# Second layer's output norms: the residual on GpSimd, sums R behind it, and another order in the last pair of tiles

## The chip, the cores and the metric

The kernel runs on one core of a Trainium2 chip. The core has five engines with a queue of instructions each: TensorE (PE in the profile, with its weight loads as PEld), VectorE (DVE), ScalarE (ACT), GpSimd (POOL) and SyncE (SP), which here only issues transfers. An engine works its queue strictly in order; an instruction waits until the semaphores it names have been raised by other engines or by transfers, and whatever stands behind it on the same engine waits too.

The metric is the device time of one execution in microseconds (us). Three runs of the kernel before took 855.74, 856.96 and 857.38 us, so the median is 856.96 us. The profiled execution took 857.13 us by the same clock, and its span from the first to the last instruction is 855.2 us.

## The reference

The input x has 4 x 512 rows of 512 numbers, that is 2048 rows, all float32. Two layers follow each other, and each adds the layer norm of its result to its own input:

```python
x = x + _layernorm(_L0_attn_ref(_layernorm(x, axis=-1), w_gate, w_up, w_down), axis=-1)
x = x + _layernorm(_L0_ffn_ref(_layernorm(x, axis=-1), W_gate, W_up, W_down), axis=-1)
```

The first layer computes `silu(x Wg^T)`, sets to zero the half of the 1376 entries of each row that are smallest in magnitude, multiplies by `x Wu^T` and by `Wd^T`. The second layer is `(silu(x Wg^T) * (x Wu^T)) Wd^T` with no selection. A layer norm takes away the row's mean and divides by the square root of its variance plus 1e-5. What the change touches is the last step of the second layer only: the layer norm of its result y, and the sum with the residual.

## The kernel before

**Tiles.** 2048 rows are 16 tiles of 128 rows. Layer 1 works on units of two tiles, layer 2 on blocks of four tiles (blocks 0 to 3), so block b has the tiles 4b to 4b+3. Products are formed with fewer matmuls than the plain way, by schemes in which sums of operands are multiplied and sums of products taken; the sums are VectorE, ScalarE and GpSimd work.

**A block of layer 2.** `Block.group` computes 128 hidden columns of gate and up for each of two halves, for each of five groups (a = 0 to 4). A group has 26 products (the table `PRODUCTS`), each of two matmuls (line 814), on six PSUM banks that are used again and again: a bank accumulates, and its running value is read after each product, by ScalarE where an output is begun (line 828) and by VectorE where it is added to (line 824). A product may not be issued into a bank before the readers of the bank's last value are done. So VectorE's place in its queue decides when TensorE may go on. Then ScalarE takes the silu (line 835) and GpSimd multiplies (line 837) and forms sums for the down projection (`down_sums`, lines 185 to 188). The last 96 hidden columns are done by `rest_sevens`; its right operands are four sums R of the block's input, made on GpSimd by `rest_right` (lines 193 to 196, about 1.27 us each), issued in the source behind group 1 of the block. R lives in the four buffers with the tag "y", which the output tiles also use.

**The down projection.** `Block.finish` calls `downs`, which takes pairs of output tiles through seven products p1 to p7, one 640 KB piece of the weights each (tag "wd", three buffers), and a short `rest` matmul pair. In blocks 0 to 2 the order is p1, p5, p6 per pair, then p7, p2, p4, p3 for both pairs together. p4 completes the two tiles yb, p3 the two tiles ya. In block 3 (`final`), p4 and p2 come per pair at the end, with p3 ahead of them for both.

**The output norm.** `out_norm` loads the residual xr (256 KB, tag "xr", two buffers), takes mean and variance (`moments`: lines 170, 172, 174 on VectorE, then `rs`, the power -1/2, on GpSimd, line 176), subtracts the mean (line 466), multiplies by `rs` and adds xr in one VectorE instruction (line 467), and issues the store of the tile (line 469). Only in the very last tile is the left half of y read straight from PSUM (`pa`, line 461).

**Who sets the order.** The source order is not the order of the queues. The block is built with `schedule_with_timeline_sim=True`: a scheduler orders each engine's instructions by its own model of time, and `tc.issue_after(i)` holds work back behind an instruction i. In the built program of before, the norms of tiles 0 and 1 of a block are interleaved on VectorE with the first additions of the next block's group 0, and on GpSimd R0 and R1 stand before the two `rs` of these norms and R2 and R3 behind them.

In the trace, tile and line names are those of the program: `yb` is an output tile of layer 2, `pab`, `pxb`, `pyb` are the six banks of a group, `padb`, `pxdb`, `pydb` the banks of the down projection.

Of the kernel before, what the change touches and what calls it, by code (L numbers as in the profile page):

```python
# [13 lines left out]
ALU = mybir.AluOpType  # L14
# [79 lines left out]
def sandwich_kernel(  # L94
# [18 lines left out]
    nc = tc.nc  # L113
# [47 lines left out]
    def bank(tag, nm):  # L161
        return psum.tile([P, 512], F32, tag=tag, name=nm)
# [165 lines left out]
    def down_right(work, key, k, w_d, nm):  # L328

        t = work.tile([P, HC, H2], F32, tag="wd", name=f"wd{nm}_{k}", bufs=3)  # L330
        raw = dict(p1=(0, 0), p2=(1, 0), p3=(1, 1))
        if k in raw:
            r, c = raw[k]
            src = w_d[r * HF : (r + 1) * HF, c * H2 : (c + 1) * H2]
            src = src.rearrange("(k p) h -> p k h", p=P)
        else:
            src = presums[key][dict(p5=1, p6=2, p7=3, p4=4)[k] - 1]
            src = src.rearrange("p (k h) -> p k h", h=H2)
        nc.sync.dma_start(t, src)
        return t  # L340

    def downs(work, pairs, key, w_d, wr, res, dst, nm, final=False):

        st = []

        ws = {}

        def begin():
            tiles, left, last = pairs[len(st)]
            pa, px, py = [bank(k, f"{k}d{nm}_{tiles[0]}")[:, :H2] for k in ("pa", "px", "py")]
            ya, yb = [
                work.tile([P, H], F32, tag="y", name=f"y{nm}_{t}", bufs=4) for t in tiles
            ]
            st.append((tiles, left, last, pa, px, py, ya, yb))

        def product(k, which, i=None, part=slice(None)):

            if k not in ws:
                ws[k] = down_right(work, key, k, w_d, f"{nm}_{pairs[0][0][0]}")
            first = i is not None
            for p in [st[i]] if first else st[part]:
                for c in range(HC):
                    nc.tensor.matmul(  # L368
                        p[which], p[1](k, c), ws[k][:, c, :],
                        start=first and c == 0, stop=c == HC - 1, skip_group_check=not first,  # L370
                    )

        def rest(ps, p, i, cols, first=False):
            nc.tensor.matmul(
                ps, p[2](i), wr[:, cols], start=first, stop=True, skip_group_check=not first
            )

        lo, hi = slice(H2), slice(H2, H)
        PA, PX, PY = 3, 4, 5
        pz = []  # L380

        def p1(i):
            begin()
            product("p1", PA, i)

        def p6(i):
            product("p6", PX, i)
            tiles, left, last, pa, px, py, ya, yb = st[i]
            nc.scalar.copy(yb[:, lo], pa)
            nc.vector.tensor_add(ya[:, hi], yb[:, lo], px)  # L390

        def p7():
            product("p7", PX)
            for p in st:
                tiles, left, last, pa, px, py, ya, yb = p
                nc.vector.tensor_add(yb[:, hi], yb[:, lo], px)  # L396
                pz.append(bank("pt", f"pz{nm}_{p[0][0]}")[:, :H2])
                rest(pz[-1], p, 1, hi, True)

        def c22():  # L400
            for p, z in zip(st, pz):
                tiles, left, last, pa, px, py, ya, yb = p
                nc.vector.tensor_add(yb[:, hi], yb[:, hi], py)
                nc.vector.tensor_add(yb[:, hi], yb[:, hi], z)

        def p2(part=slice(None)):
            product("p2", PA, None, part)
            for p in st[part]:
                tiles, left, last, pa, px, py, ya, yb = p
                rest(pa, p, 0, lo)  # L410
                if not final:
                    nc.scalar.copy(ya[:, lo], pa)
            if not final:
                c22()
            else:
                for p in st[part]:
                    tiles, left, last, pa, px, py, ya, yb = p
                    if p is st[-1]:
                        out_norm(work, tiles[0], ya, res, dst, nm, pa)
                    else:  # L420
                        nc.scalar.copy(ya[:, lo], pa)
                        out_norm(work, tiles[0], ya, res, dst, nm)

        def p4(part=slice(None)):
            product("p4", PX, None, part)
            for p in st[part]:
                tiles, left, last, pa, px, py, ya, yb = p
                rest(px, p, 1, lo)
                nc.vector.tensor_add(yb[:, lo], yb[:, lo], px)
                out_norm(work, tiles[1], yb, res, dst, nm)  # L430

        def p3(part=slice(None)):
            product("p3", PY, None, part)
            for p in st[part]:
                tiles, left, last, pa, px, py, ya, yb = p
                rest(py, p, 0, hi)
                nc.vector.tensor_add(ya[:, hi], ya[:, hi], py)
                if not final:
                    out_norm(work, tiles[0], ya, res, dst, nm)

        heads = [
            f
            for i in range(len(pairs))
            for f in (lambda i=i: p1(i), lambda i=i: product("p5", PY, i), lambda i=i: p6(i))
        ]
        if not final:
            return heads + [p7, p2, p4, p3]

        ends = [lambda f=f, i=i: f(slice(i, i + 1)) for i in range(len(pairs)) for f in (p4, p2)]
        return heads + [p7, c22, p3] + ends  # L450

    def out_norm(work, t, y, res, dst, nm, pa=None):


        xr = work.tile([P, H], F32, tag="xr", name=f"xr{nm}_{t}")
        nc.sync.dma_start(xr, res[ts(t, P), :])
        if pa is not None:
            parts = [pa, y[:, H2:]]
            mv, rs = moments(parts, f"o{nm}_{t}", "f")
            for i in range(2):  # L460
                nc.vector.tensor_scalar(
                    y[:, ts(i, H2)], parts[i], mv[:, 0:1], None, ALU.subtract
                )
        else:
            mv, rs = moments([y], f"o{nm}_{t}", "o")
            nc.vector.tensor_scalar(y, y, mv[:, 0:1], None, ALU.subtract)
        nc.vector.scalar_tensor_tensor(y, y, rs, xr, ALU.mult, ALU.add)
        queue = nc.sync if pa is None else nc.scalar
        queue.dma_start(dst[ts(t, P), :], y)

# [457 lines left out]
    def layers(nm, general):  # L928
        with ExitStack() as sctx:
            wpool = sctx.enter_context(tc.tile_pool(name="w" + nm, bufs=1))  # L930
            big = sctx.enter_context(tc.tile_pool(name="big" + nm, bufs=10))
            work = sctx.enter_context(tc.tile_pool(name="work" + nm, bufs=2))
# [28 lines left out]
            for q in range(2):  # L961
# [3 lines left out]
                t = [y[:, :, ts(q, Q)] for y in (t1, t2, t4)]  # L965
# [72 lines left out]
            for tag, n in (("wg", 43), ("wu", 43), ("wus0", 10), ("wus1", 10)):  # L1038
                n = min(n, NG * NP - len(w_of))
                t = wpool.tile([P, n, P], F32, tag=tag, name=f"{tag}2{nm}")  # L1040
                i = 0
# [7 lines left out]
            t = wpool.tile([P, 7, 2, n], F32, tag="wus2", name=f"w_rest{nm}")  # L1049
# [18 lines left out]
            for b, block in enumerate(blocks):  # L1068
                last = b + 1 == len(blocks)
                for a in range(HC):  # L1070
                    block.group(a, w_of[a * NP : (a + 1) * NP])
                    block.down_sums(a)
                    if b == 2 and a == 0 and not general:
                        nbad, loads = count_bad()
                    if b and a == 1:
                        block.rest_right()
                if b:
                    block.rest_sevens(rest_left)
                elif general:
                    block.rest(w_rest)  # L1080
                if b == 0:
                    blocks_w = [w[:, 2 * c : 2 * c + 2, :] for w in w_rest for c in range(2)]
                    with tc.issue_after(block.mark):
                        rest_left = stationary_sums(nc.vector, *blocks_w, *w_rests)
                if not last:
                    with tc.issue_after(block.mark):
                        for k in range(TB):
                            blocks[b + 1].norm(k)
                    blocks[b + 1].sums()
                with ExitStack() as order:  # L1090
                    if last and not general:
                        for i in loads:
                            order.enter_context(tc.issue_after(i))
                    block.finish([0, 1], wr, last)
# [43 lines left out]
```

## Time and profile before

| what | value |
|---|---|
| median of three runs | 856.96 us (855.74 to 857.38) |
| profiled execution, its own time | 857.13 us |
| its span | 855.2 us |
| PE busy | 839.8 us, 98% of the span |
| DVE busy | 599.5 us, 70% |
| ACT busy | 347.2 us, 41% |
| POOL busy | 167.2 us, 20% |
| output norms of layer 2, the fused VectorE multiply-add (line 467) | 16 of 0.750 us |
| the subtraction before it (line 466) | 15 of 0.477 us at the median, one of 1.425 us |
| GpSimd operation on 128 x 512 float32 (lines 193 to 196) | 12 of about 1.27 us |

A busy share is an average over stages with different limits. TensorE's busy time counts overlapping and modelled ends, so 98% does not say that it never waits: where two matmul pairs that usually start 0.43 us apart start 1 us apart, TensorE has waited. The trace's timeline gives start and duration of each instruction, and in brackets the idle time before it and what ended it.

### The profile page before, as it was taken

What the parts mean: (1) busy time and instruction counts of PE and PEld (TensorE: products, weight loads), DVE (VectorE), ACT (ScalarE), POOL (GpSimd) and SP (SyncE); (2) the same over time, 40 slices, a digit from 0 to 9 for tenths busy, and PEclk for the clock granted to TensorE, in tenths of its full rate; (3) what the DMA queues carried; (4) which work ended last, traced back from release to release, by engine and by line L of the source; (5) the groups of instructions that cost most, each with busy time, mean ns of one, the idle gap of its engine ahead of it and who ended that gap; (6) DMA issues with size and microseconds to landing.
All of it is one profiled execution on the core that took longest, in us unless ns stands there. A gap on an engine that the chain in (4) does not pass through costs nothing.

```text
span 855.2 us, 10736 instructions
## 1 busy us (share of the span) xinstructions
PE 839.8 (98%) x3550; PEld 640.8 (75%) x3550; DVE 599.5 (70%) x1679; ACT 347.2 (41%) x719; POOL 167.2 (20%) x230
## 2 busy tenths in 40 slices
PE   9999999999999999999999999999999999999996
PEld 5556566767667676677867888888888888888885
DVE  4988679796977768597867665766656665576524
ACT  3367574748466575746122331133211332033200
POOL 1000000100000100000000453154503553055401
PEclk9999999999999999999999999999999999999999
DMA  9996013727324233196466003510055001530032
GB/s 332 385 365 218 1 55 124 253 74 256 132 92 133 89 129 137 62 329 236 167 206 209 1 2 94 201 68 1 2 174 189 2 1 31 167 129 1 1 104 98
DMA packets 65393, 112.20 MB, mean 131 GB/s; under 512 B 4720, under 2 KB 44784, under 8 KB 64432
## 3 DMA queue, kind: packets, MB, share of 16 engines
q1 hardware_dynamic: 65184, 111.16, 38.2%
q8 instruction: 30, 0.49, 0.2%
q14 instruction: 35, 0.29, 0.1%
q10 hardware_dynamic: 144, 0.26, 0.1%
HBM read 90.96 MB, written 20.45 MB: 130 GB/s over the span
## 4 chain that ended last, share of the span: by engine, by line
PE 89%; DMA 3%; DVE 3%; SPq 2%; ACT 1%; issue 1%; POOL 1%; POOLq 0%; DVEq 0%; ACTq 0%
PE pg L541 15%; PE pxb L814 9%; PE pab L814 8%; PE pyb L814 8%; PE pxu L210 6%; PE pxd L368 6%; PE pxdb L368 5%; PE pyd L368 4%; PE pyu L210 4%; PE pad L368 4%; PE pau L210 4%; PE padb L368 4%; PE pydb L368 4%; PE ph L715 2%; PE pxrb L210 1%; SPq L253 1%
## 5 line engine op out<-in xcount | busy, mean ns | idle before, releaser
L593 ACT ACTIVATE ja<-v,cur 128x1376 bf16<-128x1376 f32 x96 | 138.4, 1441 | 42.7 <-DVE cur L618 32.5
L541 PE MATMUL pg<-wg,xT 128*128 128x456 f32 (+1 forms) x384 | 155.3, 549 | 0.3 <-DVE p L563 0.3
L541 PEld LDWEIGHTS pg<-wg,xT 128*128 128x128 f32 x384 | 71.9, 190 | 61.4 <-issue 56.4
L837 POOL TENSOR_TENSOR hTb<-sg,hTb 128x512 f32<-128x512 f32 x40 | 50.9, 1272 | 103.7 <-DVE hTb L824 91.7
L545 ACT ACTIVATE p<-pg 128x456 f32<-128x456 f32 (+1 forms) x48 | 26.1, 548 | 66.0 <-PE pg L541 56.6
L176 POOL TENSOR_TENSOR rs_o<-ve_o,nhalf 128x1 f32<-128x1 f32 x16 | 10.7, 682 | 188.4 <-DVE ve_o L174 188.4
L210 PE MATMUL pau<-wu,xT 128*128 128x344 f32 x128 | 43.1, 452 | 0.0
L835 ACT ACTIVATE sg<-sg 128x512 f32<-128x512 f32 x40 | 23.0, 622 | 48.5 <-DVE sg L824 48.5
L176 POOL TENSOR_TENSOR rs_i<-ve_i,nhalf 128x1 f32<-128x1 f32 x16 | 11.3, 711 | 153.8 <-DVE ve_i L174 93.2
L824 DVE TENSOR_TENSOR sg<-sg,pxb 128x256 f32<-128x256 f32 x80 | 33.6, 420 | 10.4 <-PE pxb L814 8.6
L824 DVE TENSOR_TENSOR hTb<-hTb,pab 128x256 f32<-128x256 f32 x60 | 25.1, 418 | 22.2 <-ACT sg L828 11.0
L368 PE MATMUL pad<-wd_p,hT 128*128 128x256 f32 x160 | 38.9, 380 | 0.2 <-DMA wd_p<-in_L_attn_w_down_dram 0.2
L368 PE MATMUL padb<-wdb_p,hTb 128*128 128x256 f32 x160 | 38.1, 380 | 0.6 <-DMA wdb_p<-in_L_ffn_W_down_dram 0.6
L828 ACT ACTIVATE hTb<-pab 128x256 f32<-128x256 f32 x40 | 15.3, 383 | 55.8 <-PE pab L814 50.5
L368 PE MATMUL pydb<-wdb_p,D 128*128 128x256 f32 x160 | 37.6, 379 | 0.0
L368 PE MATMUL pxd<-wd_p,hT 128*128 128x256 f32 x160 | 37.1, 380 | 0.5 <-DVE y L396 0.5
L368 PE MATMUL pxdb<-wdb_p,hTb 128*128 128x256 f32 x160 | 36.2, 379 | 0.1
L368 PEld LDWEIGHTS pxd<-wd_p,hT 128*128 128x128 f32 x160 | 30.3, 190 | 6.6 <-DVE y L396 0.9
L368 PEld LDWEIGHTS pad<-wd_p,hT 128*128 128x128 f32 x160 | 29.7, 190 | 6.9 <-issue 1.2
L720 ACT COPY hT<-ph 128x512 f32<-128x512 f32 (+1 forms) x45 | 22.6, 509 | 29.3 <-PE ph L715 23.8
L368 PEld LDWEIGHTS padb<-wdb_p,hTb 128*128 128x128 f32 x160 | 30.3, 190 | 5.2 <-DMA wdb_p<-in_L_ffn_W_down_dram 1.0
L210 PEld LDWEIGHTS pau<-wu,xT 128*128 128x128 f32 x128 | 23.8, 190 | 13.6 <-issue 4.3
(299 smaller groups left out, 1920.1 us busy)
## 6 DMA issues: line engine op xcount, KB each, us to landing
wd_p<-sum_a SPq DMA_DIRECT2D x28, 640.0 KB, 4.1
wd_p<-in_L_attn_w_down_dram SPq DMA_DIRECT2D x21, 640.0 KB, 3.9
wdb_p<-sum_f SPq DMA_DIRECT2D x16, 640.0 KB, 4.1
wdb_p<-in_L_ffn_W_down_dram SPq DMA_DIRECT2D x12, 640.0 KB, 4.1
w_ops<-area SPq DMA_DIRECT2D x4, 1664.0 KB, 6.2
xn<-in_x_dram SPq DMA_DIRECT2D x16, 256.0 KB, 4.3
xr<-in_x_dram SPq DMA_DIRECT2D x16, 256.0 KB, 4.1
x<-y SPq DMA_DIRECT2D x16, 256.0 KB, 3.3
```

Source lines behind the costliest of these rows:

```text
L176: nc.gpsimd.tensor_tensor(rs, ve, nhalf, ALU.pow)
L210: nc.tensor.matmul(ps, self.left[k][:, c, :], self.right[k][:, c, :], start=first and c == 0, stop=c == 1, skip_group_check=not first,)
L368: nc.tensor.matmul(p[which], p[1](k, c), ws[k][:, c, :], start=first and c == 0, stop=c == HC - 1, skip_group_check=not first,)
L541: nc.tensor.matmul(pg, self.xT[:, i, c, :], wg[:, c, c0:c1], start=(c == 0), stop=(c == NH - 1),)
L545: nc.scalar.activation(p[:, c0:c1], pg, AF.Silu)
L593: nc.scalar.activation(junk, v, AF.Sign, bias=cur[:, 0, i : i + 1], accum_out=cur[:, 1, i : i + 1],)
L715: nc.tensor.transpose(pt[: isz[i], c, :], h[:, i * P : i * P + isz[i]], ident)
L720: copy(hT[:, g0 : g0 + nf, :], pt[:, :nf, :])
L814: self.product = nc.tensor.matmul(banks[k], w[wv], self.left[xv], start=first, stop=True, skip_group_check=not first,).ins
L824: self.mark = add(c, c, banks[k]).ins
L835: nc.scalar.activation(sg[:, part], sg[:, part], AF.Silu)
L837: nc.gpsimd.tensor_mul(h[:, part], sg[:, part], h[:, part])
```

## The change

It has three parts.

1. In blocks 0 to 2, the norms of the two tiles that p3 completes (six tiles in all: 0, 1, 4, 5, 8, 9) are done differently (`spare`). One VectorE instruction subtracts the mean and multiplies by `rs`, in place of the subtraction alone, and the residual xr is added by GpSimd in place of VectorE's fused multiply-add. VectorE issues one instruction less for each tile, GpSimd one more. The store then waits for GpSimd. The norms of the other ten tiles stay as they were.
2. `rest_right` is held back behind the last instruction of the last output norm (`normed[-1]`). In the built program, GpSimd's order at the three boundaries is now: both `rs`, both residual sums, R0, R1, R2, R3, where it was R0, R1, both `rs`, R2, R3.
3. In block 3, p3 is no longer done for both pairs ahead of p4 and p2, but per pair: p4, p3, p2 of the first pair, then p4, p3, p2 of the second. The weights of p4 are now loaded before those of p3. In the built program TensorE does p4 of pair 0 with its rest, p3 of pair 0 with its rest, eight matmuls of p4 of pair 1, p2 of pair 0 with its rest, the end of p4 of pair 1, p3 of pair 1, p2 of pair 1. The number of matmuls is the same.

On VectorE, the part of a boundary's queue that changes is, for tiles 0 and 1 (and so for 8 and 9; at tiles 4 and 5 the addition from `pab` stands behind the norms' variances):

```
before: add pab, ve0, sub0, ve1, sub1, add pxb, add pab3, fused0, add pyb, fused1, add pxb4
after:  add pab, ve0, ve1, add pxb, add pab3, submul0, submul1, add pyb, add pxb4
```

```diff
@@ downs, p3
                 if not final:
-                    out_norm(work, tiles[0], ya, res, dst, nm)
+                    out_norm(work, tiles[0], ya, res, dst, nm, spare=key == "f")
@@ downs, order of the last block
-        ends = [lambda f=f, i=i: f(slice(i, i + 1)) for i in range(len(pairs)) for f in (p4, p2)]
-        return heads + [p7, c22, p3] + ends
-
-    def out_norm(work, t, y, res, dst, nm, pa=None):
+        ends = [
+            lambda f=f, i=i: f(slice(i, i + 1)) for i in range(len(pairs)) for f in (p4, p3, p2)
+        ]
+        return heads + [p7, c22] + ends
+
+    normed = []
+
+    def out_norm(work, t, y, res, dst, nm, pa=None, spare=False):
@@ out_norm
             mv, rs = moments([y], f"o{nm}_{t}", "o")
-            nc.vector.tensor_scalar(y, y, mv[:, 0:1], None, ALU.subtract)
-        nc.vector.scalar_tensor_tensor(y, y, rs, xr, ALU.mult, ALU.add)
+            if spare:
+                nc.vector.tensor_scalar(y, y, mv[:, 0:1], rs, ALU.subtract, ALU.mult)
+                nc.gpsimd.tensor_add(y, y, xr)
+            else:
+                nc.vector.tensor_scalar(y, y, mv[:, 0:1], None, ALU.subtract)
+        if not spare:
+            nc.vector.scalar_tensor_tensor(y, y, rs, xr, ALU.mult, ALU.add)
+        normed.append(nc.cur_bb.bb.instructions[-1])
@@ layer 2, groups of a block
                     if b and a == 1:
-                        block.rest_right()
+                        with tc.issue_after(normed[-1]):
+                            block.rest_right()
```

## The prediction

> **What bounds the kernel now.** I read the engine totals, then what TensorE waited for, and the timeline where it waited. The first lines are the page's engine totals and the trace's list of waits of PE.
>
> ```profile
> PE 839.8 (98%) x3550; PEld 640.8 (75%) x3550; DVE 599.5 (70%) x1679; ACT 347.2 (41%) x719; POOL 167.2 (20%) x230
> ...
> PE pxb L814 <- DVE hTb L824: 2.0, 3, 1.0
> PE pab L814 <- DVE hTb L824: 0.3, 1, 0.3
> ```
>
> TensorE sets the pace nearly everywhere, so an engine beside it is worth something only where TensorE waits for it. The waits listed are few, and they lie at the three boundaries between blocks, where group 0 of the next block shares VectorE with the norms. The list understates them, because the modelled end of the pair before hides part of a wait; the cadence does not. A group is 26 pairs, and between waits two pairs start 0.43 us apart: from 563.59 to 574.81 the chain shows the same pair of groups 0 and 1 of block 1, 11.22 us apart. Here is the third boundary on the timeline.
>
> ```profile
> 750.27 0.60 PE L814 MATMUL pab<-T,area 128*128 128x256 f32 x2
> ...
> 753.00 1.26 POOL L194 TENSOR_TENSOR R<-xTb,R 128x512 f32<-128x512 f32 x1 [0.65 <-DMA out_dram<-yb]
> ...
> 753.12 1.43 DVE L466 TENSOR_SCALAR yb<-yb,mv_ob 128x512 f32<-128x512 f32 x1
> ...
> 754.23 1.25 POOL L176 TENSOR_TENSOR rs_ob<-ve_ob,nhalf 128x1 f32<-128x1 f32 x2
> 754.47 0.41 DVE L824 TENSOR_TENSOR hTb<-hTb,pxb 128x256 f32<-128x256 f32 x1
> ...
> 754.93 0.70 PE L814 MATMUL pxb<-T,area 128*128 128x256 f32 x2 [1.05 <-DVE hTb L824]
> ...
> 762.81 0.59 PE L814 MATMUL pab<-T,wg 128*128 128x256 f32 x2
> ```
>
> Group 0 takes 762.81 - 750.27 = 12.54 us here, 1.32 more than 11.22. The other boundaries: 552.30 to 564.72 is 12.42 (1.20 more), 651.09 to 663.89 is 12.80 (1.58 more). In the second, a small matmul of the flags (pbad) delays two pairs by 0.21 and 0.11 us, which the change leaves, so 1.26. VectorE costs TensorE 1.20 + 1.26 + 1.32 = 3.78 us.
>
> The chain at the first boundary: the two powers on GpSimd stand behind R1, which waits for a store; VectorE stands at its first multiply-add; the addition that frees the bank pxb is behind it.
>
> ```profile
> 556.73 1.06 POOL L176 TENSOR_TENSOR rs_ob<-ve_ob,nhalf 128x1 f32<-128x1 f32 x2
> ...
> 557.31 0.75 DVE L467 SCALAR_TENSOR_TENSOR yb<-yb,rs_ob,xrb 128x512 f32<-128x512 f32 x1 [1.00 <-POOL rs_ob L176]
> ...
> 557.98 0.41 DVE L824 TENSOR_TENSOR sg<-sg,pyb 128x256 f32<-128x256 f32 x1
> ...
> 559.44 0.70 PE L814 MATMUL pxb<-T,area 128*128 128x256 f32 x2 [0.55 <-DVE hTb L824]
> ```
>
> The end of the kernel, where nothing overlaps:
>
> ```profile
> 846.25 1.00 SPq L456 DMA_DIRECT2D xrb<-x  x1
> ...
> 847.64 0.43 DVE L170 BATCH_NORM_STATS2 st_ob<-padb 128x6 f32<-128x256 f32 x1
> 848.10 0.75 DVE L467 SCALAR_TENSOR_TENSOR yb<-yb,rs_ob,xrb 128x512 f32<-128x512 f32 x1
> 848.76 0.20 DVE L172 BATCH_NORM_AGGREGATE mv_ob<-st_ob 128x2 f32<-128x12 f32 x1
> ...
> 849.90 0.75 DVE L467 SCALAR_TENSOR_TENSOR yb<-yb,rs_ob,xrb 128x512 f32<-128x512 f32 x1
> ```
>
> The last matmuls are done at 847.6; tile 15's multiply-add lies between the last tile's statistics and their aggregation.
>
> **The boundaries, part by part.** Per tile VectorE loses a subtraction (0.477 us) and a multiply-add (0.750) and gets one instruction with two row scalars. The input norms of layer 2 have that form (line 181): 0.546 at the median. So 0.68 us less for each of six tiles, 4.1 in all, but what counts is when the freed additions run. At the first boundary, with durations of before: the first variance ends at 554.79 as now; GpSimd, R gone, starts the power 0.08 later (as 549.21 to 549.29) and needs 0.53 for one (1.06 for two), so the powers end at 555.40 and 555.93. VectorE goes straight on: addition from pxb at 554.76, from pab3 at 555.10 (its product starts at 554.47 and is readable 0.63 later), the new instruction at 555.44 and 555.97, the addition from pyb near 556.4 instead of 557.98. Before, 1.46 us lay between that addition and the pair that waited for it (557.98 to 559.44), so this pair could go at 557.9; by cadence it is due at 552.30 + 14 x 0.432 = 558.35. The other wait, for the addition from pxb (before at 555.55, now 554.76, read by 555.18), is due at 555.76. Both go. The third boundary has the same times 197.97 us later. At the second the three additions from the banks move 0.66 us up, to 653.34 (654.00 before, which let a pair due at 654.00 go at 654.47; now read by 653.76), and the powers, ended near 654.4, are ready before VectorE comes at 654.53. I take the whole 3.78 us. Its ends are 3.78 and 2.0 (three lost races, first rival); I stay near the upper, because VectorE then has nothing left that is late.
>
> What the moved work meets. The two residual sums are GpSimd additions on 128 x 512, the kind and size of R0 to R3: 1.27 us each, from about 556.1 to 558.7. R0 and R1 follow, to 561.3. R2 and R3 wait for the stores of tiles 0 and 1: now issued about 557.5 and 558.8, landed 2.4 later, so R3 ends near 563.9, as before (562.57 + 1.27). Behind them wait the group's multiplication (564.19 before, could now start 1.2 earlier but does not) and the sums for the down projection; their readers are the down products some 40 us on, and R's are the matmuls from 611.1. Cover gone would cost what GpSimd lags, but it is idle most of each group. SP issues the two stores after GpSimd rather than VectorE, about when it did (558.12, 559.11); behind them stand the next residual loads and weights that nobody awaits for tens of us. ScalarE's next read of pyb stands behind VectorE's addition and moves up with it. These cost nothing.
>
> Against the move stands the Trainium skill, "GPSIMD Engine Reference", section "Engine selection": elementwise work belongs on VectorE, GpSimd being about twice as slow with two inputs. The rows agree on the speed (1.27 against 0.75), and by that rule each tile would cost 0.52 more, 3.1 us in all; nobody on TensorE's path waits for these tiles, so I give it nothing.
>
> **The last pair.** TensorE's matmuls are the same number in another order. p4 gets the earlier load (issued 824.73, about 4 us, needed at 831.88), p3 the later one (826.89, needed after 12 matmuls, 834.5), p2 the third (831.64, lands near 835.8, needed at 838.8): no wait. Tile 15's sum is complete after 12 + 12 + 8 + 12 + 4 matmuls at 0.216 us, 842.45, so its norm is done by about 846.6, and the last tile's aggregation follows its statistics at 848.1 instead of 848.76: up to 0.67 us. But the last residual load has two buffers, so it waits for tile 12's multiply-add, which comes near 845.0 (845.05 before); issued at 846.2, landing 3.3 later as this load did, it is there at 849.5, against a multiply-add that could start at 849.23. Landings of these two loads were 2.6 and 3.3 us. The ends are 0 (all else hidden) and 0.67; I take 0.4, by the same load's own row.
>
> **Sum.** 3.78 + 0.4 = 4.18 us off the profiled 857.13 gives 852.95. That execution is 0.17 above the median of the runs, so the median would be 852.8.
>
> **The rivals.**
>
> *GpSimd gets in first.* At 753.12 the subtraction took 1.43 us instead of 0.48, because R1 had begun 0.12 earlier; it ended 0.29 after R1. At 555.41 it was the other way: R1 took 1.36 and the subtraction, 0.25 ahead, its 0.48. The second new instruction has the form of that subtraction, and the first residual sum becomes ready just as it does: VectorE waits for the second power (555.93 + 0.04), GpSimd for the first new instruction (555.99 + 0.08). The margin is 0.10 us, 0.18 at the second boundary. If GpSimd wins, VectorE stands until 556.07 + 1.27 + 0.29 = 557.63, the addition from pyb starts at 557.55, the pair goes near 558.95 instead of 558.35: 0.6 us. At the first and third boundary together 1.2: 854.0; at all three 1.8: 854.6. The Trainium skill, "SBUF — State Buffer", section "Who interferes with whom", gives the rule: VectorE in a two-port mode and GpSimd share a port pair under an exclusive lock, and whichever issues first blocks the other for the whole instruction. The two rows agree with it.
>
> *The norms are not what TensorE waits for.* If another step of group 0 (ScalarE's reads, which stand in the same chain) held these pairs, 3.78 us would stay and the time be 856.5, within 0.2%. Against it: ScalarE's late read at 558.42 waited for VectorE.
>
> *Slower: the sums block the bank additions.* Six GpSimd operations now run without gaps where four ran with them. If each also stopped VectorE's additions from PSUM, each boundary would stand 2 x 1.27 us longer while losing nothing: 3 x 2.54 = 7.6, 860.4. It decides as soon as these additions take longer than 0.42 us. Against it: over all 360 of them the longest is 0.423, and those beside R2 at 560.35 are no longer.
>
> **How the numbers follow.** My case 45%; a lost race at one or two boundaries 33% (up to 854.0), at all three 7% (854.6); unchanged 7%; slower 4% for the blocked additions and 4% for what I do not see. The range: the top is three lost races and nothing at the end (857.0 - 2.0 = 855.0); the bottom the full 4.45 us and the 0.5 us by which runs lie below their median: 852.0. It leaves out about 15%. 0.2% (1.7 us) is about what a measurement of this kernel can tell from no change; the first three cases are faster by more: 0.85 and a little of the fourth.
>
> **What would show it.** Group 0 of blocks 1 to 3 at 11.2, 11.6 and 11.2 us; powers right behind the variances; the new instruction at 0.55, or one of each two near 1.8 where the race is lost; additions from PSUM still 0.42; the last aggregation near 848.1 - 3.8. It is wrong if TensorE in group 0 waits for VectorE as long as before, or if a later group or down product begins to wait for GpSimd.

## The result, and the profile after

The changed kernel took 854.38 us in the median of 12 runs (853.83 to 855.74), the kernel before 856.90 us in 12 runs beside it. The ratio is 0.9972, with a 95% interval of 0.9964 to 0.9980: faster, by 2.5 us. The forecast was 852.8 with a range of 852.0 to 855.0. The profiled execution took 854.17 us, its span is 852.4 us.

First the engine totals on the page of the kernel after, then its list of what PE waited for (us in total, times, longest).

```profile
PE 839.4 (98%) x3550; PEld 641.6 (75%) x3550; DVE 597.6 (70%) x1673; ACT 347.5 (41%) x719; POOL 174.1 (20%) x236
```

```profile
PE pxb L824 <- DVE hTb L834: 0.9, 2, 0.5
```

VectorE has six instructions less and GpSimd six more, as the change says. The waits of PE for VectorE in group 0 went from four to two. Which two were left is in the timeline of the kernel after: the first boundary, the second, the third, and the end.

```profile
554.55 1.21 POOL L176 TENSOR_TENSOR rs_ob<-ve_ob,nhalf 128x1 f32<-128x1 f32 x2 [4.34 <-DVE ve_ob L174]
...
555.18 2.22 DVE L471 TENSOR_SCALAR yb<-yb,mv_ob,rs_ob 128x512 f32<-128x512 f32 x2
...
555.86 1.27 POOL L472 TENSOR_TENSOR yb<-yb,xrb 128x512 f32<-128x512 f32 x1
...
557.33 0.41 DVE L834 TENSOR_TENSOR sg<-sg,pyb 128x256 f32<-128x256 f32 x1
...
558.66 0.70 PE L824 MATMUL pxb<-T,area 128*128 128x256 f32 x2 [0.47 <-DVE hTb L834]
...
653.84 1.00 DVE L471 TENSOR_SCALAR yb<-yb,mv_ob,rs_ob 128x512 f32<-128x512 f32 x2
...
654.51 2.69 POOL L472 TENSOR_TENSOR yb<-yb,xrb 128x512 f32<-128x512 f32 x2 [0.91 <-ACT sg L838]
...
748.24 0.60 PE L824 MATMUL pab<-T,area 128*128 128x256 f32 x2
...
751.44 2.22 DVE L471 TENSOR_SCALAR yb<-yb,mv_ob,rs_ob 128x512 f32<-128x512 f32 x2
...
752.11 1.27 POOL L472 TENSOR_TENSOR yb<-yb,xrb 128x512 f32<-128x512 f32 x1
...
760.20 0.59 PE L824 MATMUL pab<-T,wg 128*128 128x256 f32 x2
...
843.52 0.42 SPq L460 DMA_DIRECT2D xrb<-x  x1
...
845.50 0.21 DVE L172 BATCH_NORM_AGGREGATE mv_ob<-st_ob 128x2 f32<-128x12 f32 x1
...
846.97 0.75 DVE L476 SCALAR_TENSOR_TENSOR yb<-yb,rs_ob,xrb 128x512 f32<-128x512 f32 x1 [0.42 <-DMA xrb<-x]
```

Read the pairs of line 471. At all three boundaries GpSimd's first sum begins 0.67 to 0.68 us after the first new instruction. At the second boundary the two new instructions take 1.00 us together, at the first and third 2.22 us. Narrower windows on the same timeline show the single instructions: the second power and the second new instruction at the first boundary, and the second new instruction at the second boundary.

```profile
555.06 0.70 POOL L176 TENSOR_TENSOR rs_ob<-ve_ob,nhalf 128x1 f32<-128x1 f32 x1
...
555.79 1.61 DVE L471 TENSOR_SCALAR yb<-yb,mv_ob,rs_ob 128x512 f32<-128x512 f32 x1
...
654.30 0.54 DVE L471 TENSOR_SCALAR yb<-yb,mv_ob,rs_ob 128x512 f32<-128x512 f32 x1
```

At the first boundary the second new instruction waits for the second power, starts about 0.06 us before GpSimd's sum (555.79 against 555.86) and ends 0.28 us after it. At the third it is the same (752.05 against 752.11). At the second boundary it starts 0.22 us before the sum and takes 0.54 us. The powers now stand right behind the variances everywhere. The table has the length of group 0, from its first matmul to the first of group 1 (steady groups take 11.22 us), and the end, from the first matmul of p4 of the last two tile pairs to the start of the last multiply-add.

| stretch, us | before | after | forecast |
|---|---|---|---|
| group 0 of block 1 | 12.42 | 11.97 | 11.2 |
| group 0 of block 2 (0.32 of it the flags' matmul) | 12.80 | 11.55 | 11.6 |
| group 0 of block 3 | 12.54 | 11.96 | 11.2 |
| the end | 18.02 | 17.69 | 17.6 |

Together 0.45 + 1.25 + 0.58 + 0.33 = 2.61 us, against 2.8 us in the two spans and 2.5 us in the medians. What is missing against the forecast of 4.2 lies at the first and third boundary.

### The profile page after: what moved, and what is told of

It reads as the page before. It is cut to its first block, busy times and chain, and to the rows that moved or that the text cites. A ratio compares the mean times of both kernels' runs of the same rounds, so it can differ in the third digit from the quotient of the medians.

```text
span 852.4 us, 10727 instructions
## 1 busy us (share of the span) xinstructions
PE 839.4 (98%) x3550; PEld 641.6 (75%) x3550; DVE 597.6 (70%) x1673; ACT 347.5 (41%) x719; POOL 174.1 (20%) x236
## 4 chain that ended last, share of the span: by engine, by line
PE 84%; DVE 5%; DMA 3%; ACT 3%; SPq 2%; issue 1%; POOL 0%; ACTq 0%; DVEq 0%; POOLq 0%
PE pg L551 13%; PE pxb L824 9%; PE pab L824 9%; PE pyb L824 8%; PE pxdb L368 5%; PE pxd L368 5%; PE pxu L210 5%; PE padb L368 4%; PE pydb L368 4%; PE pyd L368 4%; PE pyu L210 3%; PE pau L210 3%; PE pad L368 3%; ACT ja L603 3%; PE ph L725 1%; DMA xnb<-x 1%
## 5 line engine op out<-in xcount | busy, mean ns | idle before, releaser
L834 DVE TENSOR_TENSOR hTb<-hTb,pyb 128x256 f32<-128x256 f32 x60 | 25.3, 421 | 12.3 <-PE pyb L824 11.8
```

What stands on the lines that cost most here:

```text
L834: self.mark = add(c, c, banks[k]).ins
```

## The experiments

Two theories were in question. The port theory: GpSimd's first residual sum gets ahead of VectorE's second new instruction at a port that both need, and VectorE stands until it is done. Its rival: the second instruction is late because its power is late. Beside that, the parts of the change were run apart: the last pair, the residual on GpSimd, and R in two places other than the change's own (right behind the powers, and far behind the boundary). R in its own place, behind the last norm instruction, was not run without the residual sums. The times stand against runs of the kernel before on the same chip.

**The residual sums in the other order** (on the changed kernel). GpSimd works in order, so with the second tile's sum first, none can begin before VectorE's second instruction is done.

```diff
-                nc.gpsimd.tensor_add(y, y, xr)
+                def add():
+                    with tc.issue_after(normed[-1]):
+                        normed.append(nc.gpsimd.tensor_add(y, y, xr).ins)
+                    nc.sync.dma_start(dst[ts(t, P), :], y)
+                return add
@@ p3, behind its loop over the tiles
+            for add in reversed(adds):
+                if add is not None:
+                    add()
```

> The changed kernel, but GpSimd adds the residual of the second tile first, so its first sum cannot be ready before VectorE's second new instruction is done; every other instruction keeps its place. Port theory (GpSimd's first sum takes the shared port and stops VectorE's second subtract-and-multiply): each pair of these instructions takes about 1.0 to 1.1 us at all three boundaries instead of 2.22, 1.00, 2.22; group 0 of blocks 1, 2, 3 takes 11.2, 11.6, 11.2 us instead of 11.97, 11.55, 11.96; the time is about 1.5 us below 854.4, so 852.9. Rival (the second instruction is late because its power is late, whoever holds the port): pairs stay near 2.2 and groups near 11.97 at the first and third boundary, the time at 854.4.

Measured: 852.44 us against 856.72, ratio 0.9947 (0.9934 to 0.9961); group 0 of 11.23, 11.54 and 11.22 us. The timeline of this run at the first boundary:

```profile
554.81 1.22 POOL L176 TENSOR_TENSOR rs_ob<-ve_ob,nhalf 128x1 f32<-128x1 f32 x2 [4.34 <-DVE ve_ob L174]
...
555.45 1.16 DVE L475 TENSOR_SCALAR yb<-yb,mv_ob,rs_ob 128x512 f32<-128x512 f32 x2
...
556.52 0.41 DVE L844 TENSOR_TENSOR sg<-sg,pyb 128x256 f32<-128x256 f32 x1
...
556.74 2.50 POOL L479 TENSOR_TENSOR yb<-yb,xrb 128x512 f32<-128x512 f32 x2 [0.71 <-ACT sg L848]
```

The powers take as long as before the repair (1.22 against 1.21 us), and still the pair of new instructions takes 1.16 us, so the rival falls: a late power is worth the 0.16 us above the 1.00 us of the second boundary, and TensorE does not feel it. Its list of waits has none for VectorE in group 0 any more. In the trace every engine has the same kinds of instructions in the same order as after the change; what differs is which tile's sum, and with it which store, comes first. So GpSimd's sum beside the second new instruction is what cost the 0.75 and 0.74 us that the change left at the first and third boundary. The run shows that the sum stops the instruction; that they meet at a port is the theory's reason for it.

**The order of the last pair alone** (on the kernel before).

```diff
-        ends = [lambda f=f, i=i: f(slice(i, i + 1)) for i in range(len(pairs)) for f in (p4, p2)]
-        return heads + [p7, c22, p3] + ends
+        ends = [
+            lambda f=f, i=i: f(slice(i, i + 1)) for i in range(len(pairs)) for f in (p4, p3, p2)
+        ]
+        return heads + [p7, c22] + ends
```

> The kernel before with the new order of the last pair alone. Measured from the first matmul of p4 of the last pair's first half to the start of the last multiply-add: 18.02 us before, 17.69 after the whole change. Theory (the order gains by itself, and the last residual load then holds the end): 17.7, with the last multiply-add waiting for the load; group 0 of blocks 1 to 3 stays at 12.4, 12.8, 12.5; the time is 0.3 below before, too little for the runs to tell. Rival (the end gained because of the boundaries' changed stores): 18.0.

Measured: 856.52 us against 856.72, ratio 0.9995 (0.9986 to 1.0005), so the runs can't tell it from before. The trace can: the end took 17.71 us (832.50 to 850.21).

```profile
846.75 0.73 SPq L458 DMA_DIRECT2D xrb<-x  x1
...
850.21 0.75 DVE L469 SCALAR_TENSOR_TENSOR yb<-yb,rs_ob,xrb 128x512 f32<-128x512 f32 x1 [0.43 <-DMA xrb<-x]
```

The last multiply-add waits for its residual, as after the whole change. The order is worth 0.3 us by itself in this execution. Group 0 took 12.61, 12.62 and 12.60 us here, a little otherwise than in the profile of before though no instruction there differs, with a sum within 0.1 us of that of before. The rows show one cause: R1, which waits for a transfer, came first against the second subtraction at the first boundary too (1.49 us), where in the profile of before it did so at the third alone.

**R behind the powers** (on the kernel before). GpSimd's R0 to R3 stand behind the two powers of the boundary; VectorE keeps its subtractions and fused multiply-adds. The scheduler moved more than R, though: at the first and third boundary the addition from pyb now stands behind both fused multiply-adds, where it stood between them, and the additions behind it and two reads on ScalarE changed places.

```diff
+        power = nc.gpsimd.tensor_tensor(rs, ve, nhalf, ALU.pow).ins
+        if kind != "i":
+            out_powers.append(power)
...
-                        block.rest_right()
+                        with tc.issue_after(out_powers[-1]):
+                            block.rest_right()
```

> The kernel before with the sums R held behind the two powers on GpSimd, and nothing else: VectorE keeps its subtraction and its fused multiply-add. Theory (half of the boundary's loss was the powers waiting behind R1): powers right behind the variances, addition from pyb near 557.6 in place of 557.98, group 0 of 11.9, 12.2, 11.9 us instead of 12.42, 12.80, 12.54; time about 1.6 us below before, 855.3. Rival (VectorE's work is what counts, R's place does not): 12.4, 12.8, 12.5 and the time of before. Other rival (R's place was all of it): 11.2, 11.6, 11.2 and 853.2.

Measured: 862.34 us against 856.72, ratio 1.0063 (1.0048 to 1.0078): slower by 5.6 us where I expected 1.6 faster, and group 0 took 15.48, 13.46 and 15.48 us. None of the three expectations holds. The timeline at the first boundary:

```profile
555.10 1.24 POOL L178 TENSOR_TENSOR rs_ob<-ve_ob,nhalf 128x1 f32<-128x1 f32 x2 [4.34 <-DVE ve_ob L176]
...
556.31 1.26 POOL L197 TENSOR_TENSOR R<-xTb 128x512 f32<-128x512 f32 x1
...
556.45 3.35 DVE L471 SCALAR_TENSOR_TENSOR yb<-yb,rs_ob,xrb 128x512 f32<-128x512 f32 x2
...
557.65 1.59 POOL L198 TENSOR_TENSOR R<-xTb,R 128x512 f32<-128x512 f32 x1
```

The powers are early, as expected. But R0 begins 0.14 us before the first fused multiply-add, R1 gets between the first and the second, and the pair takes 3.35 us, where a pair without R beside it takes 1.41 (the next run). So the fused form, which reads two tiles from SBUF, seemed to be stopped as the subtractions were; I had priced the port only for the forms with one tile. That called for the next run.

**R far from the boundary** (on the kernel before). The built order of TensorE, VectorE and ScalarE is the same as in the run above; only R is held behind the down sums of group 1.

```diff
                     if b and a == 1:
-                        block.rest_right()
+                        behind = next(
+                            i for i in reversed(nc.cur_bb.bb.instructions)
+                            if i.engine == mybir.EngineType.Pool
+                        )
+                        with tc.issue_after(behind):
+                            block.rest_right()
```

> The kernel before with the sums R held behind the down sums of group 1, so some 22 us after the boundary. VectorE's queue at the boundary is that of the run with R right behind the powers (subtractions and fused multiply-adds kept), only R is gone from beside it. Theory (there R0 and R1 stopped the fused multiply-adds, which read two tiles from SBUF, at the shared port): the pair of fused multiply-adds takes 1.41 us again instead of 3.35, group 0 takes about 11.9, 12.1, 11.9 instead of 15.48, 13.46, 15.48, and the time is about 1.9 us below before, 855.0. Rival (the multiply-adds were late for another reason, their residual loads or the powers): 3 us again and groups of 13 to 15, slower than before. If the groups come to 11.2, 11.6, 11.2, the instruction that the change saves on VectorE was worth nothing.

Measured: 855.50 us against 856.62, ratio 0.9987 (0.9977 to 0.9996); group 0 of 12.27, 12.11 and 12.27 us.

```profile
554.63 1.24 POOL L176 TENSOR_TENSOR rs_ob<-ve_ob,nhalf 128x1 f32<-128x1 f32 x2 [4.34 <-DVE ve_ob L174]
...
555.98 1.41 DVE L467 SCALAR_TENSOR_TENSOR yb<-yb,rs_ob,xrb 128x512 f32<-128x512 f32 x2
...
557.30 0.41 DVE L824 TENSOR_TENSOR sg<-sg,pyb 128x256 f32<-128x256 f32 x1
...
559.05 0.70 PE L814 MATMUL pxb<-T,area 128*128 128x256 f32 x2 [0.41 <-DVE hTb L824]
```

With R gone the pair takes 1.41 us, so it was R, beside the same instructions in the same order, that stopped the fused multiply-adds. The gain is 1.1 us, where I expected 1.9: the groups at the first and third boundary are 0.37 us longer than I expected, the one at the second is as expected. This run leaves 2.67 us of the 3.78 (12.27 + 12.11 + 12.27 less 11.22 + 11.54 + 11.22). Not all of that is the length of VectorE's norm instructions. At the first and third boundary the addition that frees pxb stands behind one more addition in the order that the scheduler made, and starts 1.28 us after the addition from pyb; at the second, where the order is that of before, it is 0.86 us. The difference, 0.42 us, is about what these two groups took too long. No run has early powers with the old order; by this estimate some 0.6 us at each boundary would be left, and the reversed sums, with less work on VectorE, come to 11.2.

**The residual on GpSimd, and nothing else** (on the changed kernel, with R and the last pair put back).

```diff
-                        with tc.issue_after(normed[-1]):
-                            block.rest_right()
+                        block.rest_right()
@@ downs: the order of the last pair as before the change
```

> The residual on GpSimd and one VectorE instruction less, with R left where it was and the last pair's order of before. Theory (without moving R the powers stay late, and VectorE then also loses the port to the first residual sum): first new instruction near 557.3 at the first boundary, the second near 2 us behind it, group 0 of about 12.7, 12.9, 12.4 us, no gain: the time within 1 us of before. Rival (two instructions of 0.75 us less on VectorE gain by themselves): group 0 of 11.9, 12.2, 11.9 and about 1.6 us below before.

Measured: 856.66 us against 856.72, ratio 1.0002 (0.9993 to 1.0011); group 0 of 12.71, 12.55 and 12.52 us, 37.78 in all against 37.76 before.

```profile
556.04 1.17 POOL L176 TENSOR_TENSOR rs_ob<-ve_ob,nhalf 128x1 f32<-128x1 f32 x2
...
556.63 0.55 DVE L469 TENSOR_SCALAR yb<-yb,mv_ob,rs_ob 128x512 f32<-128x512 f32 x1 [1.52 <-POOL rs_ob L176]
...
557.31 1.27 POOL L470 TENSOR_TENSOR yb<-yb,xrb 128x512 f32<-128x512 f32 x1
...
557.42 1.44 DVE L469 TENSOR_SCALAR yb<-yb,mv_ob,rs_ob 128x512 f32<-128x512 f32 x1
...
559.24 0.70 PE L822 MATMUL pxb<-T,area 128*128 128x256 f32 x2 [1.21 <-DVE hTb L832]
```

The powers stand behind R1 again, VectorE waits 1.52 us for the first, and the second new instruction, which starts 0.8 us behind the first and not 2 as I expected, loses to the first residual sum, 1.44 us instead of 0.55. The instruction that VectorE saves is eaten by these two: no gain, as the theory said. The addition from pyb stands between the two new instructions here and behind both after the change.

**The last residual early** (on the changed kernel). The last tile's residual gets one of the input tiles' buffers.

```diff
-        xr = work.tile([P, H], F32, tag="xr", name=f"xr{nm}_{t}")
+        kw = {} if pa is None else dict(bufs=3)
+        tag = "xr" if pa is None else "xn"
+        xr = work.tile([P, H], F32, tag=tag, name=f"xr{nm}_{t}", **kw)
```

> The changed kernel with the last tile's residual in a buffer of its own (one of those of the input tiles, free by then), so that its load no longer waits for tile 12's multiply-add. Theory (after the change the last multiply-add waits for this load): it starts 0.04 us after its power, 17.35 us after the first matmul of p4 of the last pair's first half instead of 17.69; the boundaries stay at 11.97, 11.55, 11.96; the time is 0.3 below 854.4. Rival (something else holds the end, and the load only comes last by chance): 17.6 to 17.7.

Measured: 854.19 us against 857.06, ratio 0.9967 (0.9955 to 0.9979). Its interval takes in the ratio of the change itself. The end took 17.37 us (829.84 to 847.21), the boundaries 11.97, 11.54 and 11.96.

```profile
836.21 0.42 SPq L462 DMA_DIRECT2D xrb<-x  x1
...
847.21 0.75 DVE L478 SCALAR_TENSOR_TENSOR yb<-yb,rs_ob,xrb 128x512 f32<-128x512 f32 x1
```

The wait is gone and the end is 0.32 us shorter, as expected: after the change the load was what came last. The time is too small a step for the runs.

**Both repairs together.** The sums reversed and the last residual early.

> The changed kernel with both repairs: the second tile's residual sum first on GpSimd, and the last residual load early. If the port and the load are the two things that the change left, group 0 of blocks 1 to 3 takes 11.2, 11.6, 11.2 us, the end 17.35, and the time is 1.8 us below 854.4, about 852.6, which is what was forecast for the change itself. If either is not, its part stays: 854.1 with the first alone missing, 852.9 with the second.

Measured: 852.68 us against 857.06, ratio 0.9949 (0.9935 to 0.9962); group 0 of 11.23, 11.54 and 11.22 us, the end 17.36. Its interval lies below that of the change (0.9964 to 0.9980), and it is where the forecast put the change, by two edits that the change does not have. It is not told apart from the reversed sums alone (0.9947), where in the profiled execution the last load landed only after 3.8 us and the end took 18.19, longer than the 18.02 of before: the early load takes away a wait that was 0.4 to 0.9 us long.

## Why the prediction was right, and where it was short

*The direction, and the range: right.* The prediction saw 3.78 us of TensorE's waiting at the three boundaries as VectorE's doing, and these stretches are where most of the gain came from. The run with the sums reversed shows that the 3.78 us were all there to be had: its groups are at 11.23, 11.54 and 11.22.

*"I take the whole 3.78 us": wrong, 2.28.* This is the step that failed. I let the margins between VectorE's and GpSimd's start, 0.10 us at the first and third boundary and 0.18 at the second, go to VectorE at all three, and at the first and third VectorE lost. The first rival described it with the right place and nearly the right price: 0.6 us forecast at each of the two, 0.75 and 0.74 measured; 854.0 us forecast, 854.38 measured. (Its own terms, 557.55 and the 1.46 us used before, give 559.01 and not 558.95, so 0.66 us.) It had a third of the chance and was the case. The time fell into the range because the range was drawn wide enough for three lost races.

*Why the margin went the other way.* I let the two powers end at 0.53 us each. At the second boundary they did, 1.06 us for both. At the first and third they took 1.21 and 1.22 us, because the second power took 0.70 us while the first new instruction ran beside it. So VectorE's second instruction started 0.61 us behind its first instead of 0.46, and its lead over GpSimd's sum was 0.06 us instead of 0.22. (GpSimd began 0.13 us after the end of the first new instruction, where I had 0.08.) The trace of before had the sign of it: at 549.29 a power beside a subtraction took 0.81 us, and the 1.06 us that I used was of a pair with a fused multiply-add beside it. Over all nine traces, each power of layer 2's output norms took 0.54 to 0.56 us, also beside a fused multiply-add, and 0.61 us or more where a subtraction, or the new instruction, ran beside it for 0.29 us or longer. No run was made for this alone. How much lead VectorE needs stays open: by the starts in the trace it was 0.06 us ahead and lost, and it won with 0.22 us here and with 0.24 us in the trace of before, so two recorded starts 0.06 us apart do not say which engine goes first.

*The second boundary: right.* The margin, 0.18 us forecast and 0.22 in the trace, was enough: 11.55 us against 11.6 forecast.

*The last pair: right, and by the row that was taken.* 0.33 us against 0.4. The last aggregation came 0.66 us earlier within the end, as forecast; the upper value, 0.67, was held back by the last residual's load, which landed 3.3 us after its issue as in the profile of before. The run with the early load shows the rest: 18.02 - 17.37 = 0.65. That the load took 3.3 us again is luck in part: in the profile of the reversed sums it took 3.8 us, and nothing of the gain was left.

*What was costed at nothing: right.* GpSimd's R3 ended 11.89 us after the start of group 0 at the first boundary (562.59 + 1.28 - 551.98), forecast 11.6, and no wait of PE for GpSimd's sums or for R came up. The additions from PSUM, on which the slower rival rested, stayed at 0.423 us at most beside GpSimd's six operations in a row.

*What the prediction did not see.* It priced parts 1 and 2 together and did not say how much each needs the other. The residual on GpSimd alone changed the time by 0.02%, which the runs can't tell from nothing; R right behind the powers made the kernel 0.63% slower; R far from the boundary made it 0.13% faster. Taking the multiply-add away paid only with R no longer ahead of the powers, and R beside the fused multiply-adds cost more than early powers gain.

## What to carry to other kernels

When work moves from VectorE to GpSimd, look at what VectorE does in the microsecond when GpSimd starts, not only at how long GpSimd takes: here 0.7 us at each of two places hung on a lead of 0.06 us in place of 0.22, and turning the order of two sums round gave it back. Put GpSimd's work behind the last VectorE instruction that it could stop, by a dependency and not by a hope about times. When two edits share an engine's queue, price them together, since each alone may be worth nothing or cost more than both gain. And compare the built order of every engine before a run is called a test of one thing: here holding back R also changed the order of VectorE's additions.

## What the runs showed of the hardware

- VectorE's fused multiply-add with two tiles in SBUF is stopped by a GpSimd addition beside it, and stops it: 3.35 us for a pair instead of 1.41, with R1 at 1.59 instead of 1.27. The Trainium skill, "SBUF — State Buffer", section "Who interferes with whom", states this for VectorE instructions with two SBUF inputs against GpSimd instructions that read SBUF, and states that an instruction with at most one SBUF input outside the two-port modes does not contend; the runs agree with both, the second by 0.423 us as the longest of the 360 additions from PSUM.
- A 128 x 1 power of layer 2's output norms on GpSimd took 0.54 to 0.56 us, and 0.61 to 1.03 us where a VectorE subtraction, or subtract-and-multiply, of an output tile ran beside it for 0.29 us or longer. A fused multiply-add beside it did not lengthen it (0.54 to 0.55 us).
- The same subtract-and-multiply on 128 x 512 took 0.54 us where GpSimd's sum began 0.22 us or more after it (with the sums reversed all six took 0.540 to 0.547), 1.61 us where the sum began 0.06 us after it, and 1.44 us where the sum had begun 0.11 us before it (the residual on GpSimd alone). The row of the kernel after:

```profile
L471 DVE TENSOR_SCALAR yb<-yb,mv_ob,rs_ob x6: 541/542/1612, 555.2 to 752.1; 128x512 f32<-128x512 f32 x6
```
